# A graph layer on one core: rows of some chunks loaded one by one by two engines instead of one, and other sizes of the last node blocks

## The chip, the cores and the metric

The kernel runs on one core of one Trainium2 chip. The core has five engines, each with its own stream of instructions: TensorE (PE in the profile; PEld are its weight loads), VectorE (DVE), ScalarE (ACT), GpSimd (POOL) and SyncE (SP). SP computes nothing; it issues DMAs. ACT and POOL can issue DMAs as well. An instruction waits on semaphores, and what stands behind it on the same engine waits with it. The metric is the device time in microseconds (us); smaller is better.

## The reference, cut to what matters

There are N = 12500 nodes with D = 128 features and E = 200000 edges, sorted by destination. H is 512.

```python
h = jnp.maximum(_layernorm(x, axis=-1), 0.0)
msgs = h[src]                                            # one row of h per edge
agg = jax.ops.segment_sum(msgs, dst, num_segments=n)     # summed by destination
deg = jax.ops.segment_sum(jnp.ones((src.shape[0],), h.dtype), dst, num_segments=n)
agg = agg / jnp.maximum(deg, 1.0)[:, None]
y = jax.nn.relu(agg @ Wg + h @ Ws + bg)
y = jnp.tanh(y @ W1 + b1)
y = jnp.tanh(y @ W2 + b2)
out = x + (y @ W3 + b3)
```

Everything is float32.

## The kernel before

**Setup.** In nine pieces x is loaded, normalised on VectorE and ScalarE, and stored as the table `htab` in DRAM (lines 217 to 235). The edge lists are loaded, turned on TensorE and kept as one column per chunk: `scol` (sources) and `dloc` (destinations less the start of a window). GpSimd meanwhile runs 80 indirect DMAs of raw rows of x (line 142), which need no `htab`; these rows are normalised later on their own.

**Chunks.** The edges are cut into NCH = 1563 chunks of 128. A chunk's 128 source rows must be in SBUF, one per partition. They come in one of three ways:

- raw: 80 chunks, the gathers of line 142 from x;
- `gather(c)` (line 297): one indirect DMA on GpSimd from `htab`, with the indices of `scol[:, c]`. These chunks are listed in `order` (line 587), and 32 buffers (`AHEAD`) let it run 32 chunks ahead;
- slow: the chunks in the list `slow` (lines 84 to 91), one in every 81 that are not raw, from chunk 160. `row_loads` (line 314) loads their rows one by one: it reads 16 addresses from the tile `place` into registers of SP (line 320) and issues 16 DMAs of one 512-byte row each (line 327). It is a generator, and one call of `next(loading, 0)` in the main loop (line 639) issues one such batch of 16. Two buffers (`rows_one`) hold such chunks.

The addresses in `place` come from small loads of `src`, one per slow chunk, on ScalarE's queue (line 310).

**Sums.** As the destinations are sorted, chunk c touches only nodes near 8 * c. `window(c)` gives the start and the width of the window that its destinations must fall in (`WINDOWS`, line 49, narrower near the end). VectorE makes a one-hot matrix for eight chunks at a time (`onehot`, line 357), and `add(c)` (line 407) multiplies the rows by it on TensorE and sums into a block of nodes. A chunk that reaches two blocks is summed in `edge` first and handed to both by `merge`. One output, `flag`, says whether some destination fell outside its window; in that case `general`, a slower path, computes all again.

**Blocks and layers.** The nodes are cut into blocks (lines 103 to 107): 23 of 512, one of 256, three of 128 and a last one of 84. Once all chunks that reach a block are added, its dense layers can run: `part0` (agg and own rows through Wg and Ws, ReLU), `part1` (W1, tanh), `part2` (W2, tanh), `part3` (W3), `part4` (turned back, plus x, stored). They are generators as well.

**Order.** TensorE's instructions are kept in the order in which the code writes them (class `pe`, line 282), and so are SP's DMAs in the main loop (`sp_dma`). The main loop (line 616) goes over the chunks. For each it issues gathers up to 32 ahead, perhaps a batch of row loads, and `add(c)`. Up to chunk `QUICK` = 1376 it then does one step of the layers at every second chunk. From there on a small plan (`costs`, `soonest`, `go_on`, and `there`, the time at which a chunk's rows are expected) decides how many steps stand between two chunks. A block's layers begin `lead` chunks after its last chunk when it shares chunks with the next block: ten (`LEAD`) before `QUICK`, two after it. ScalarE's instructions are not held in written order.

Of the kernel before, what the change touches and what calls it, by code (L numbers as in the profile page):

```python
# [22 lines left out]
F32 = mybir.dt.float32  # L23
# [3 lines left out]
AF = mybir.ActivationFunctionType  # L27
# [4 lines left out]
P = 128  # L32
EPS = 1e-5
CPR = 16
BLK = 512
# [4 lines left out]
STEP = 40  # L40
AHEAD = 32
SLOW0 = 160
EACH = 80
LOADS = 16
LATE = 12
LEAD = 10
QUICK = 1376

WINDOWS = ((0, 144), (1496, 88), (1536, 56))
W_RAW = 160  # L50
W_MAX = max(W_RAW, *(w for _, w in WINDOWS))

# [6 lines left out]
def windowed(ctx, tc, x, src, dst, Wg, Ws, bg, W1, b1, W2, b2, W3, b3, out, flag):  # L59
    nc = tc.nc  # L60
    N, D = x.shape
# [9 lines left out]
    NCH = -(-E // P)  # L71
# [4 lines left out]
    assert D == P and H % P == 0 and per * E == N * P and RAW0 % GRP == STEP % GRP == 0  # L76
    assert all(c % GRP == 0 for c, _ in WINDOWS) and RAW1 <= WINDOWS[1][0]


    def raw(c):  # L80
        return RAW0 <= c < RAW1 and (c - RAW0) % STEP < GRP


    slow, n = [], 0
    for c in range(SLOW0, NCH - 100):
        if not raw(c):
            if n == 0:
                slow.append(c)
                n = EACH
            else:  # L90
                n -= 1


    def first(w, span=per):
# [6 lines left out]
        return per * c + first(w), w  # L101

    blocks, n = [], 0
    for w in [BLK] * (N // BLK - 1) + [BLK // 2] + [P] * 3:
        blocks.append((n, w))
        n += w
    blocks.append((n, N - n))

    dram = ctx.enter_context(tc.tile_pool(name="dram", bufs=1, space=bass.MemoryType.DRAM))
    const = ctx.enter_context(tc.tile_pool(name="const", bufs=1))  # L110
    raws = ctx.enter_context(tc.tile_pool(name="raws", bufs=1))
    rows_one = ctx.enter_context(tc.tile_pool(name="rows_one", bufs=2))
# [10 lines left out]
    for t, a in ((rsrc, src), (rdst, dst)):  # L123
        a = a[RAW0 * P : RAW1 * P].rearrange("(u e) -> u e", u=NRAW)[:, : GRP * P]
# [14 lines left out]
    for g in range(NRAW):  # L139
        t = raws.tile([P, GRP, D], F32, name=f"raw{g}")  # L140
# [44 lines left out]
    with tc.tile_pool(name="setup", bufs=1) as sp, tc.tile_pool(name="ln", bufs=2) as ln:  # L185
# [58 lines left out]
        )  # L244
        for c0, w in WINDOWS[1:]:
            v = low[:, c0:]
# [19 lines left out]
    bgc = const.tile([P, 1], F32, name="bgc")  # L266
    nc.scalar.dma_start(bgc, bg.rearrange("(p o) -> p o", o=1))
    b1c = const.tile([P, HM], F32, name="b1c")
    b2c = const.tile([P, HM], F32, name="b2c")
# [3 lines left out]
    b3c = const.tile([P, 1], F32, name="b3c")  # L273
# [20 lines left out]
    def sp_dma(*a):  # L294
        tc.keep_in_program_order(nc.sync.dma_start(*a))
# [10 lines left out]
    ROWB = 4 * D  # L306
    hbytes = htab.rearrange("n d -> (n d)").bitcast(U8)
# [3 lines left out]
    place = const.tile([len(slow), P], I32, name="place")  # L311
    nc.vector.tensor_scalar(place, at_i, float(ROWB), None, op0=ALU.mult)

    def row_loads():
        for i, c in enumerate(slow):
            r = rows_one.tile([P, D], F32, name="srows")
            rows_t[c] = r
            rb = r.bitcast(U8)
            for p0 in range(0, P, LOADS):
                loads, vs = nc.values_load_multi_w_load_instructions(  # L320
                    place[i : i + 1, p0 : p0 + LOADS], engines=[mybir.EngineType.SP], min_val=0, max_val=(N - 1) * ROWB,
                    skip_runtime_bounds_check_because="src holds rows of x, as the indirect DMAs take it to",
                )
                for ld in loads:
                    tc.keep_in_program_order(ld)
                for p, v in enumerate(vs, p0):
                    sp_dma(rb[p : p + 1, :], hbytes[bass.ds(v, ROWB)].rearrange("(o b) -> o b", o=1))
                yield

    def raw_stats(i):  # L330
        return stats_raw[:, :, i * GRP : (i + 1) * GRP]
# [39 lines left out]
    for c in range(NCH):  # L371
        lo, w = window(c)
# [28 lines left out]
    edge = {}  # L401
# [5 lines left out]
    def add(c):  # L407
        rows, oh = rows_t.pop(c), ohs[c // GRP][:, c % GRP]
        lo, w = window(c)
        b = min(b for b, cs in enumerate(reach) if c in cs)  # L410
        n, m = blocks[b]
        if c in across[b]:
            e0, e1 = edge_span(b)
            if c == across[b][0]:
                edge[b] = ps_b.tile([P, BLK], F32, name="edge")
            pe.matmul(
                edge[b][:, lo - e0 : lo - e0 + w], rows, oh[:, :w], start=(c == across[b][0]),
                stop=(c == across[b][-1]), skip_group_check=True,
            )
            if c == across[b][-1]:  # L420
                sums = ed.tile([P, BLK], F32, name="sums", bufs=2)
                nc.scalar.copy(sums[:, : e1 - e0], edge.pop(b)[:, : e1 - e0])
                edges[b] = sums
            return
        a0, a1 = max(lo, n), min(lo + w, n + m)
        if b not in acc:
            acc[b] = ps_a.tile([P, BLK], F32, name="agg")
            start = True
        else:
            start = False  # L430
        pe.matmul(
            acc[b][:, a0 - n : a1 - n], rows, oh[:, a0 - lo : a1 - lo], start=start,
            stop=(c == inside[b][-1] and not across[b]), skip_group_check=True,
        )
# [29 lines left out]
    def own_turned(s):  # L464

        k = -(-min(BLK, N - s * BLK) // P)
        hb = owns.pop(s)
        pt = ps_t.tile([P, BLK // P, P], F32, name="pt")
        for t in range(k):
            pe.transpose(pt[:, t, :], hb[:, t, :], ident)  # L470
        hT = ml.tile([P, BLK], F32, name="hT")
        nc.scalar.copy(hT[:, : k * P], pt[:, :k, :].rearrange("p t n -> p (t n)"))  # L472
        hTs[s] = hT

    def own_part(b):
# [15 lines left out]
    h0s, h1s, h2s, h3s = {}, {}, {}, {}  # L491
# [9 lines left out]
    def part0(b):  # L501
        n, mm, hop = costs(b)
        s, off = divmod(blocks[b][0], BLK)
        if n == BLK:
            own_part(b)
        yield 0, 0
        mT = ml.tile([P, BLK], F32, name="mT")
        nc.vector.tensor_tensor(mT[:, :n], acc[b][:, :n], rds.pop(b)[:, :n], op=ALU.mult)  # L508
        yield mm, 0
        p0 = flat(ps_m.tile([P, 4, P], F32, name="pm"))  # L510
        pe.matmul(p0[:, :n], ws, hTs[s][:, off : off + n], start=True, stop=False)
        yield mm, n / 90
        pe.matmul(p0[:, :n], wg, mT[:, :n], start=False, stop=True)
        h0s[b] = ml.tile([P, BLK], F32, name="h0")
        nc.scalar.activation(h0s[b][:, :n], p0[:, :n], AF.Relu, bias=bgc)  # L515

    def part1(b, spread):
        n, mm, hop = costs(b)
        size, bufs = wide(b)
        h0, h1s[b] = h0s.pop(b), ml.tile([P, HM, size], F32, name=f"h1_{size}", bufs=bufs)  # L520
        for m in range(HM):
            if spread and m > 1:
                yield 0, 0
            yield mm, hop if m == 0 else 0
            p1 = flat(ps_m.tile([P, 4, P], F32, name="pm"))
            pe.matmul(p1[:, :n], w1[:, m * P : (m + 1) * P], h0[:, :n], start=True, stop=True)
            nc.scalar.activation(h1s[b][:, m, :n], p1[:, :n], AF.Tanh, bias=b1c[:, m : m + 1])  # L527

    def part2(b):
        n, mm, hop = costs(b)  # L530
        size, bufs = wide(b)
        h1, h2s[b] = h1s.pop(b), ml.tile([P, HM, size], F32, name=f"h2_{size}", bufs=bufs)
        for m in range(HM):
            p2 = flat(ps_m.tile([P, 4, P], F32, name="pm"))
            for kk in range(HM):
                yield mm, hop if m == 0 and kk == HM - 1 else 0
                pe.matmul(
                    p2[:, :n], w2[:, kk, m * P : (m + 1) * P], h1[:, kk, :n], start=(kk == 0), stop=(kk == HM - 1)
                )
            nc.scalar.activation(h2s[b][:, m, :n], p2[:, :n], AF.Tanh, bias=b2c[:, m : m + 1])  # L540

    def part3(b):
        n, mm, hop = costs(b)
        h2 = h2s.pop(b)
        p3 = flat(ps_m.tile([P, 4, P], F32, name="pm"))
        for kk in range(HM):
            yield mm, hop if kk == HM - 1 else 0
            pe.matmul(p3[:, :n], w3[:, kk, :], h2[:, kk, :n], start=(kk == 0), stop=(kk == HM - 1))
        h3s[b] = ml.tile([P, BLK], F32, name="h3", bufs=1)
        nc.scalar.activation(h3s[b][:, :n], p3[:, :n], AF.Identity, bias=b3c)  # L550

    def part4(b):
        n0, (n, mm, hop) = blocks[b][0], costs(b)
# [31 lines left out]
        )  # L585

    order = [c for c in range(NCH) if not raw(c) and c not in slow]
    loading = row_loads()
    work, done, nxt, behind = [], 0, 0, 0
    ngrp = -(-NCH // GRP)  # L590
    span = BLK // per
# [24 lines left out]
    for c in range(NCH):  # L616
# [18 lines left out]
        if not raw(c) and c not in slow:  # L635
            behind += 1
            batch = behind * P // (EACH * LOADS)
            if behind > SLOW0 - 2 * EACH and batch > (behind - 1) * P // (EACH * LOADS):
                next(loading, 0)
        if c >= QUICK:  # L640

            there = 7.5 + 1.251 * (NRAW * GRP + order.index(c)) if c not in slow else 0
            while soonest() and max(now, soonest()[2]) < there:
                go_on(soonest())
            now = max(now, there) + 0.27
# [402 lines left out]
```

## Time and profile before

Three runs of the kernel took 1956.88 to 1958.13 us.

| what | us |
|---|---|
| median of three runs | 1957.18 |
| the profiled execution, by its own clock | 1961.69 |
| span of its trace, first to last instruction | 1959.50 |
| GpSimd busy | 1465.9 |
| TensorE busy | 1393.8 |
| VectorE busy | 1068.2 |
| ScalarE busy | 231.8 |
| one gather of line 299, mean | 0.946 |

All lines come from one profiled execution. A line of a group of instructions reads: source line, engine, operation, tiles written and read, count; then busy time in all and the mean of one in ns; then how long the engine sat idle just before these instructions, and what ended most of that. A line of the time line reads: start and length in us, engine, line, operation, and in square brackets the idle time before it with what ended it. An engine's name with a q, as in SPq, means its instruction queue: there the issue of DMAs is shown, which is not counted as busy. A row of digits cuts the span into 40 slices, and each digit is a share in tenths.

### The profile page before, as it was taken

The numbers are of one execution on the slowest core, as the hardware profiler recorded it, in microseconds if no ns is written. First come the engines' busy times: TensorE is split into PE (matmuls) and PEld (weight loads), VectorE is DVE, ScalarE is ACT, GpSimd is POOL, SyncE is SP. The second block draws the span as 40 slices with busy tenths as digits, with TensorE's granted clock in tenths as the row PEclk, the third lists the DMA queues.
The fourth block names the chain that finished last, engine by engine and source line by source line (L and its number), as shares of the span: only waits on it lengthen the run. The fifth ranks groups of instructions, "written<-read, shape, count | busy, mean of one in ns | idle before, by whom it ended". The sixth has DMA issues, their size and how long they took to land.

```text
span 1959.5 us, 19291 instructions
## 1 busy us (share of the span) xinstructions
PE 1393.8 (71%) x5213; PEld 824.1 (42%) x5213; DVE 1068.2 (55%) x650; ACT 231.8 (12%) x364; POOL 1465.9 (75%) x1555
## 2 busy tenths in 40 slices
PE   0056677777788778877777777777677677778897
PEld 0034344444454445533443434444343333454566
DVE  6974775555667656645545545455454554545430
ACT  1100211011111111010110110110001101101122
POOL 7777777777777777777777777777777777777774
PEclk9999778899989998899989888889889898879697
DMA  7822222222222222222222222222222222222221
GB/s 195 232 69 64 54 64 65 59 70 69 59 65 70 66 74 54 70 70 53 71 59 65 69 53 70 65 59 70 59 65 64 60 70 59 71 69 69 56 61 40
DMA packets 123684, 139.31 MB, mean 71 GB/s; under 512 B 32558, under 2 KB 97978, under 8 KB 123372
## 3 DMA queue, kind: packets, MB, share of 16 engines
q0 software_dynamic: 49504, 101.48, 20.4%
q1 hardware_dynamic: 70870, 33.19, 6.2%
q10 hardware_dynamic: 3192, 3.32, 0.6%
q8 instruction: 43, 0.70, 0.2%
q14 instruction: 75, 0.61, 0.1%
HBM read 125.05 MB, written 12.82 MB: 70 GB/s over the span
## 4 chain that ended last, share of the span: by engine, by line
DMA 36%; issue 28%; PE 26%; POOL 7%; DVE 3%; ACT 0%; SPq 0%; ACTq 0%; POOLq 0%; DVEq 0%
DMA rows<-htab,scol 34%; PE pm L286 13%; PE agg L286 9%; POOL rows L299 7%; PE edge L286 3%; DMA xt<-in_x_dram 2%; PE pt L289 1%; DMA at_i<-in_src_dram 0%; DVE oh L357 0%; DVE agg L176 0%; DVE h L183 0%; DVE agg L172 0%; DVE xt L173 0%; DVE cnt L367 0%; DVE shared L176 0%
## 5 line engine op out<-in xcount | busy, mean ns | idle before, releaser
L299 POOL DMA_INDIRECT rows<-htab,scol x1467 | 1387.6, 946 | 447.5 <-issue 269.3
L286 PE MATMUL agg<-oh,rows 128*128 128x144 f32 (+3 forms) x2096 | 560.2, 365 | 335.2 <-DMA rows<-htab,scol 324.3
L286 PEld LDWEIGHTS agg<-oh,rows 128*128 128x128 f32 x2096 | 381.9, 223 | 714.1 <-DMA rows<-htab,scol 597.5
L286 PE MATMUL pm<-h,w 128*128 128x512 f32 (+3 forms) x1344 | 639.0, 573 | 1.1 <-ACT h L515 0.7
L357 DVE TENSOR_TENSOR oh<-shared,dloc 128x1152 f32<-128x1152 f32 (+2 forms) x186 | 243.9, 1318 | 542.0 <-PE agg L286 330.6
L367 DVE TENSOR_REDUCE cnt<-oh 128x200 bf16<-128x1600 f32 (+2 forms) x186 | 524.3, 2824 | 4.6
L286 PE MATMUL edge<-oh,rows 128*128 128x144 f32 (+2 forms) x838 | 212.2, 346 | 124.3 <-DMA rows<-htab,scol 123.8
L286 PEld LDWEIGHTS edge<-oh,rows 128*128 128x128 f32 x838 | 145.0, 210 | 277.1 <-DMA rows<-htab,scol 242.3
L286 PEld LDWEIGHTS pm<-h,w 128*128 128x128 f32 x1344 | 219.8, 202 | 15.2 <-issue 12.0
L540 ACT ACTIVATE h<-pm,b2c 128x512 f32<-128x512 f32 (+3 forms) x112 | 70.9, 633 | 554.8 <-PE pm L286 554.8
L527 ACT ACTIVATE h<-pm,b1c 128x512 f32<-128x512 f32 (+3 forms) x112 | 70.5, 633 | 237.4 <-PE pm L286 236.9
L142 POOL DMA_INDIRECT raw<-in_x_dram,rsrc x80 | 77.4, 967 | 25.5 <-issue 23.8
L394 DVE RECIPROCAL rd<-rd 128x512 f32<-128x512 f32 (+3 forms) x28 | 81.8, 2920 | 0.0
L564 DVE TENSOR_TENSOR o<-pt,xb 128x512 f32<-128x512 f32 x23 | 15.9, 690 | 95.7 <-PE pt L289 91.9
L508 DVE TENSOR_TENSOR mT<-agg,rd 128x512 f32<-128x512 f32 (+3 forms) x28 | 17.4, 620 | 86.6 <-PE agg L286 86.6
L201 PE MATMUL pm<-ident,idx_f 98*128 98x98 f32 x32 | 6.2, 376 | 64.2 <-DVE idx_f L197 57.8
L392 DVE TENSOR_SCALAR rd<-pm 128x512 f32<-128x512 f32 (+3 forms) x28 | 17.4, 622 | 61.6 <-PE pm L286 61.6
L515 ACT ACTIVATE h<-pm,bgc 128x512 f32<-128x512 f32 (+3 forms) x28 | 17.7, 633 | 271.8 <-PE pm L286 271.8
L472 ACT COPY hT<-pt 128x512 f32<-128x512 f32 (+1 forms) x25 | 14.4, 578 | 258.5 <-PE pt L289 246.9
L286 PE MATMUL pm<-hT,ws 128*128 128x512 f32 (+3 forms) x56 | 41.2, 831 | 0.0
L550 ACT ACTIVATE h<-pm,b3c 128x512 f32<-128x512 f32 (+3 forms) x28 | 17.7, 633 | 181.9 <-PE pm L286 181.9
L289 PE MATMUL pt<-ident,hb 128*128 128x128 f32 x98 | 16.6, 297 | 31.5 <-DMA srows<-htab 31.5
(69 smaller groups left out, 499.1 us busy)
## 6 DMA issues: line engine op xcount, KB each, us to landing
srows<-htab SPq DMA_DIRECT2D x2048, 0.5 KB
rows<-htab,scol POOLq DMA_INDIRECT x1467, 2.5
hb<-htab SPq DMA_DIRECT2D x24, 256.0 KB
xb<-in_x_dram SPq DMA_DIRECT2D x23, 256.0 KB
out_dram<-o SPq DMA_DIRECT2D x23, 256.0 KB
htab<-h SPq DMA_DIRECT2D x6, 896.0 KB
xt<-in_x_dram SPq DMA_DIRECT2D x5, 896.0 KB
raw<-in_x_dram,rsrc POOLq DMA_INDIRECT x80, 3.9
```

The source lines that it names most:

```text
L142: nc.gpsimd.indirect_dma_start(out=t[:, j, :], out_offset=None, in_=x, in_offset=bass.IndirectOffsetOnAxis(ap=rsrc[:, g, j : j + 1], axis=0),)
L286: tc.keep_in_program_order(nc.tensor.matmul(*a, **k))
L289: tc.keep_in_program_order(nc.tensor.transpose(*a, **k))
L299: nc.gpsimd.indirect_dma_start(out=r, out_offset=None, in_=htab, in_offset=bass.IndirectOffsetOnAxis(ap=scol[:, c : c + 1], axis=0),)
L357: nc.vector.tensor_tensor(oh[:, :k, :w], lane[:, None, :w].to_broadcast([P, k, w]), dloc[:, g * GRP : g * GRP + k][:, :, None].to_broadcas ...
L367: nc.vector.tensor_reduce(cnt[:, :n], shifted, AX.X, ALU.add)
L392: nc.vector.tensor_scalar(rd[:, :m], dg[:, :m], 1.0, None, op0=ALU.max)
L394: nc.vector.reciprocal(rd[:, :m], rd[:, :m])
L515: nc.scalar.activation(h0s[b][:, :n], p0[:, :n], AF.Relu, bias=bgc)
L527: nc.scalar.activation(h1s[b][:, m, :n], p1[:, :n], AF.Tanh, bias=b1c[:, m : m + 1])
L540: nc.scalar.activation(h2s[b][:, m, :n], p2[:, :n], AF.Tanh, bias=b2c[:, m : m + 1])
L550: nc.scalar.activation(h3s[b][:, :n], p3[:, :n], AF.Identity, bias=b3c)
```

## The change

1. **Two lists of slow chunks.** `slow` becomes `slow_s` (for SP, one in every 77) and `slow_a` (for ScalarE, one in every 121, up to `QUICK`). SP's list now goes on to 12 chunks before the end, not 100.
2. **ScalarE loads rows.** `row_loads` takes the list, the engine, the function that issues a DMA, the name of the tile, and how many loads go out per call. For SP this is 16 as before; for ScalarE four (`TOGETHER`), with addresses still read 16 at a time. The main loop calls ScalarE's generator in its own rhythm.
3. **ScalarE's order is held.** A class `act` keeps its activations, copies and row loads of the main loop in written order.
4. **Other last blocks.** The last blocks are 256, 128, 128, 112 and 100 instead of 256, 128, 128, 128 and 84, and from chunk 1552 on the window is 40 wide instead of 56.

```diff
-EACH = 80
+EACH = 76
+EACH_A = 120
+TOGETHER = 4
...
-WINDOWS = ((0, 144), (1496, 88), (1536, 56))
+WINDOWS = ((0, 144), (1496, 88), (1536, 56), (1552, 40))
...
-    slow, n = [], 0
-    for c in range(SLOW0, NCH - 100):
-        if not raw(c):
-            if n == 0:
-                slow.append(c)
-                n = EACH
-            else:
-                n -= 1
+    slow_s, slow_a = [], []
+    ns, na = 0, EACH // 2
+    for c in range(SLOW0, NCH - 12):
+        if raw(c):
+            continue
+        if ns <= 0:
+            slow_s.append(c)
+            ns = EACH
+        elif na <= 0 and c < QUICK:
+            slow_a.append(c)
+            na = EACH_A
+        else:
+            ns -= 1
+            na -= 1
+    slow = slow_s + slow_a
...
-    for w in [BLK] * (N // BLK - 1) + [BLK // 2] + [P] * 3:
+    for w in [BLK] * (N // BLK - 1) + [BLK // 2] + [P] * 2 + [P - 16]:
...
+    class act:
+        def activation(*a, **k):
+            tc.keep_in_program_order(nc.scalar.activation(*a, **k))
+        def copy(*a):
+            tc.keep_in_program_order(nc.scalar.copy(*a))
+        def dma(*a):
+            tc.keep_in_program_order(nc.scalar.dma_start(*a))
-    def row_loads():
-        for i, c in enumerate(slow):
-            r = rows_one.tile([P, D], F32, name="srows")
+    def row_loads(chunks, engine, dma, name, together):
+        for c in chunks:
+            i = slow.index(c)
+            r = rows_one.tile([P, D], F32, name=name)
...
-                    sp_dma(rb[p : p + 1, :], hbytes[bass.ds(v, ROWB)].rearrange("(o b) -> o b", o=1))
-                yield
+                    dma(rb[p : p + 1, :], hbytes[bass.ds(v, ROWB)].rearrange("(o b) -> o b", o=1))
+                    if (p + 1) % together == 0:
+                        yield
...
-    loading = row_loads()
+    loading = row_loads(slow_s, mybir.EngineType.SP, sp_dma, "srows", LOADS)
+    loading_a = row_loads(slow_a, mybir.EngineType.Activation, act.dma, "arows", TOGETHER)
...
+            batch = behind * P // (EACH_A * TOGETHER)
+            if behind > 48 and batch > (behind - 1) * P // (EACH_A * TOGETHER):
+                next(loading_a, 0)
```

The activations and copies of the layers (lines 422, 472, 515, 527, 540 and 550) call `act.activation` and `act.copy` in place of the engine's own.

More of the change, by code (lines that the diff above doesn't have):

```diff
@@ L107, in windowed @@
     blocks.append((n, N - n))
+    assert 0 < N - n <= P
     dram = ctx.enter_context(tc.tile_pool(name="dram", bufs=1, space=bass.MemoryType.DRAM))
@@ L320, in row_loads @@
                 loads, vs = nc.values_load_multi_w_load_instructions(
-                    place[i : i + 1, p0 : p0 + LOADS], engines=[mybir.EngineType.SP], min_val=0, max_val=(N - 1) * ROWB,
+                    place[i : i + 1, p0 : p0 + LOADS], engines=[engine], min_val=0, max_val=(N - 1) * ROWB,
                     skip_runtime_bounds_check_because="src holds rows of x, as the indirect DMAs take it to",
@@ L421, in add @@
                 sums = ed.tile([P, BLK], F32, name="sums", bufs=2)
-                nc.scalar.copy(sums[:, : e1 - e0], edge.pop(b)[:, : e1 - e0])
+                act.copy(sums[:, : e1 - e0], edge.pop(b)[:, : e1 - e0])
                 edges[b] = sums
@@ L471, in own_turned @@
         hT = ml.tile([P, BLK], F32, name="hT")
-        nc.scalar.copy(hT[:, : k * P], pt[:, :k, :].rearrange("p t n -> p (t n)"))
+        act.copy(hT[:, : k * P], pt[:, :k, :].rearrange("p t n -> p (t n)"))
         hTs[s] = hT
@@ L514, in part0 @@
         h0s[b] = ml.tile([P, BLK], F32, name="h0")
-        nc.scalar.activation(h0s[b][:, :n], p0[:, :n], AF.Relu, bias=bgc)
+        act.activation(h0s[b][:, :n], p0[:, :n], AF.Relu, bias=bgc)
     def part1(b, spread):
@@ L526, in part1 @@
             pe.matmul(p1[:, :n], w1[:, m * P : (m + 1) * P], h0[:, :n], start=True, stop=True)
-            nc.scalar.activation(h1s[b][:, m, :n], p1[:, :n], AF.Tanh, bias=b1c[:, m : m + 1])
+            act.activation(h1s[b][:, m, :n], p1[:, :n], AF.Tanh, bias=b1c[:, m : m + 1])
     def part2(b):
@@ L539, in part2 @@
                 )
-            nc.scalar.activation(h2s[b][:, m, :n], p2[:, :n], AF.Tanh, bias=b2c[:, m : m + 1])
+            act.activation(h2s[b][:, m, :n], p2[:, :n], AF.Tanh, bias=b2c[:, m : m + 1])
     def part3(b):
@@ L549, in part3 @@
         h3s[b] = ml.tile([P, BLK], F32, name="h3", bufs=1)
-        nc.scalar.activation(h3s[b][:, :n], p3[:, :n], AF.Identity, bias=b3c)
+        act.activation(h3s[b][:, :n], p3[:, :n], AF.Identity, bias=b3c)
     def part4(b):
```

## The prediction

> **What bounds the kernel now.** I read the busy shares first, then the groups of instructions, then the time line of GpSimd and of the end.
>
> ```profile
> PE 1393.8 (71%) x5213; PEld 824.1 (42%) x5213; DVE 1068.2 (55%) x650; ACT 231.8 (12%) x364; POOL 1465.9 (75%) x1555
> ...
> DMA  7822222222222222222222222222222222222221
> ...
> L299 POOL DMA_INDIRECT rows<-htab,scol x1467 | 1387.6, 946 | 447.5 <-issue 269.3
> ```
>
> GpSimd is 75% busy, but the third line says why that is full: each of its 1467 gathers takes 946 ns and is followed by 447.5 / 1467 = 305 ns in which nothing can start. "issue" as the largest releaser means that it waited for nothing that the profile shows. Does it ever wait for a free buffer? The first and the last gather of the time line answer:
>
> ```profile
> 98.46 0.95 POOL L142 DMA_INDIRECT raw<-in_x_dram,rsrc  x1 [0.31 <-DMA htab<-h]
> ...
> 104.73 0.95 POOL L299 DMA_INDIRECT rows<-htab,scol  x1 [0.30 <-DVE cnt L367]
> 105.98 0.95 POOL L299 DMA_INDIRECT rows<-htab,scol  x1 [0.30 <-issue]
> ...
> 1938.59 0.95 POOL L299 DMA_INDIRECT rows<-htab,scol  x1 [0.30 <-POOLq L1014]
> ```
>
> (1938.59 - 104.73) / 1466 = 1.2509 us a gather, and the longest single step between two gathers in the trace is 1.27 us. So GpSimd never waits, from the raw gathers before 104.73 to the last. The reader is to see that the whole kernel is one queue of gathers with a start before it and a tail behind it. TensorE follows 2.5 us behind each gather, with buffers for 32 of them.
>
> **Gathers taken off GpSimd.** Working through the loop that fills the lists of row-by-row chunks gives 16 chunks before; after, 17 on the sync engine and 9 on ScalarE, 26 together. The sum of chunks is 1563, of which 80 are raw: 1563 - 80 - 26 = 1457 gathers against 1467. Ten fewer at 1.2509 us are **-12.5 us**, all of it on the path that sets the end.
>
> Here a rule of the Trainium skill speaks against the change: "DMA: Bandwidth & Descriptors", section "Rules for kernel authors", says that spreading DMAs over SP, ACT and GpSimd brings no bandwidth, as all run on the same 16 engines; it saves issue time only. If the transfers were the bound, the gain would be 0. The row for DMA above shows 2 tenths busy after the start, and issue time is what GpSimd is full of, so the exception in that rule is this case: 12.5 us, not 0.
>
> **What ScalarE gets.** 9 x 128 = 1152 loads of one 512-byte row, four at a time, 288 batches between chunks 48 and 1225 of the loop. No row load of ScalarE is in this trace; the nearest row is the sync engine's:
>
> ```profile
> 786.99 0.41 SPq L295 DMA_DIRECT2D out_dram<-o  x1
> 789.29 11.63 SPq L295 DMA_DIRECT2D srows<-htab  x32
> 801.02 0.40 SPq L295 DMA_DIRECT2D hb<-htab  x1
> ```
>
> 32 loads with one read of addresses take 11.63 us, 0.363 each; so 1152 take 418 us, 1.45 a batch. The other end is ScalarE's 16 loads of index rows at the start (33.92 to 45.40 us, 0.72 each, under full DMA traffic): 829 us. I take 0.363, since these loads lie in the stage with little traffic. ScalarE has 231.8 us of work in 1959, so it has room. What matters is who waits for ScalarE meanwhile. Queued behind a batch are its copies and activations, and behind those TensorE. In the list of waits for TensorE between 700 and 1100 us no wait for ScalarE exists:
>
> ```profile
> PE agg L286 <- DMA rows<-htab,scol: 73.1, 104, 2.1
> PE edge L286 <- DMA rows<-htab,scol: 26.5, 35, 2.3
> PE agg L286 <- DVE oh L357: 1.5, 1, 1.5
> PE agg L286 <- DVE o L564: 0.5, 1, 0.5
> ```
>
> The code says how far that carries: up to chunk 1376 one step of the layers is issued every two chunks (2.5 us), a result of ScalarE is read three or more steps later, an edge sum ten chunks later. A batch of 1.45 us fits in that. What is still late is bought back: TensorE is busy 895.7 of the 1200 us from 300 to 1500, a quarter free, and GpSimd feels nothing until TensorE is 32 x 1.25 - 2.5 = 37 us behind. Cost **0**. Without this cover it would be the 418 us, less 25% idle time over the some 1470 us of that stage (373) and the 37 of buffers: 8. Behind chunk 1225 ScalarE has no loads, so the tail is clean.
>
> A wait comes with it. Each DMA of SP and of ACT names one of the same eight semaphores in turn and waits until the eighth DMA before it, whosever it was, has landed. Eight of SP's loads take 8 x 0.323 = 2.6 us and none waits in the row above, so a row lands within that; the gathers land in 2.5. ScalarE can thus stand up to about 2.5 us behind SP's batch, at most once for each of SP's 17 x 8 = 136 batches, and SP can't run far ahead of ScalarE. Below: no wait, since SP's program is ahead of TensorE's; above: 136 x 2.5 = 340 us on ScalarE. I take 0 on the path, by the same cover.
>
> **SP's share**, 17 chunks instead of 16, spaced 76 instead of 80: 128 x 0.363 = 46 us of loading in 76 x 1.25 = 95. Their last load lies 70 chunks and more ahead of use. Nothing.
>
> **The start.** Ten more of the small index loads on ScalarE's queue stand ahead of work of the normalisation. At their median, 0.26, they are 2.7 us; at 0.72 they are 7.2, and one more turn of the eight semaphores (one such wait lasted 3.9 us, to 38.39) makes 11. The last store to htab had landed by 98.7, while GpSimd was on raw gathers until 104.73: 6.0 us are free. Loss 0 to 5; I take **0**.
>
> **The tail.** Narrower windows from chunk 1552 let the second-last block (112 nodes) end its chunks at 1551 instead of 1554.
>
> ```profile
> 1943.72 0.30 PE L286 MATMUL agg<-oh,rows 128*128 128x28 f32 x2
> 1943.83 1.64 PEld L286 LDWEIGHTS pm<-h,w 128*128 128x128 f32 x14
> ...
> 1944.06 0.25 DVE L508 TENSOR_TENSOR mT<-agg,rd 128x84 f32<-128x84 f32 x1 [8.78 <-PE agg L286]
> ...
> 1946.80 5.79 PE L286 MATMUL pm<-h,w 128*128 128x84 f32 x48
> ```
>
> The last chunk had landed by 1938.59 + 2.5 = 1941.1, yet TensorE adds it at 1943.7 and begins the last block's hidden layers at 1946.80, 8.2 us after the last gather began, because the block before stands ahead in its order. Working the written order out again with the new reaches, that block's products all stand ahead of the last chunk's, and after it comes only the last block: 2.5 landing, 0.43 for the add, 0.3 for mT, 0.35 for wg, 0.4 for ReLU and its hand-over, 4.1 us in all with 0.1 for gaps. Gain 8.2 - 4.1 = 4.1. The clock stood at half from 1931.8 to 1942.0; should it stand so there again, the block before ends some 1 us late (gain 3), and where the old kernel ran at full clock there, its own lead was some 2.5 us shorter (gain 1.5). I take **-3.0**. The last block is 100 wide instead of 84: its 48 matmuls are bound by weight loads (1.64 / 14 = 117 ns at 128 columns, 5.79 / 48 = 121 at 84), four activations in series grow by 0.015 each: **+0.1**. Sixteen fewer columns for eleven chunks: nothing (0.30 us at 28 columns, 0.31 at 36).
>
> **Sum.** -12.5 - 3.0 + 0.1 = -15.4. The profiled execution took 1961.69 (span 1959.50 and 2.19 around it), so it would take 1946.3. The runs shown have a median 4.5 below it; off 1957.18 it is **1941.8 us**, 0.8% less.
>
> **Rivals.** (1) The start is late: 11 us against 6.0 free, a loss of 5, **1947**. For it: one such semaphore wait already stands there; against it: DVE has idle time there as well. (2) The clock is halved under the last 48 matmuls (ten took 2.46 at half clock, so 11.8 instead of 5.7): **1948**. For it: 22% of the trace is at half clock; against: TensorE is steadily busy just before. (3) Row loads slow GpSimd's gathers by 10 ns each: 1457 x 10 = 14.6, **1956**, no change. Against: the pitch was 1.2510 with SP's loads about and 1.2506 after they ended at 1680. (4) ScalarE becomes the bound, **slower**: 418 us of issue and 340 of semaphore waits all stop TensorE: 758 - 373 - 37 = 348, less 15.4, about **2290**. It decides from 425 us on TensorE's path, 1.48 a batch. For it: TensorE's order is fixed, and one late result stops all chunks behind it; against: the list of waits. That the change fails to do what it says, a destination outside a 40-wide window so that the general path runs as well, is out: in the drawn inputs the nearest destination lies 14 nodes inside.
>
> **Numbers.** Forecast 0.68 (own range 1939 to 1944.5), (1) 0.12, (2) 0.07, (3) 0.04, (4) 0.09. A measurement of this kernel tells 0.2%, 3.9 us, from no change. Faster: 0.68 + 0.10 of (1) + 0.07 = 0.85; same: 0.02 of (1) and 0.03 of (3) = 0.05; slower: 0.01 of (3) and (4) = 0.10. The range takes in (1) and (2): 1938.5 to 1949; what it leaves out are (3) and (4) and edges.
>
> **What would show it.** Right: 1457 gathers at 1.251 us, the first at 104.7, the last at 1926.1; 1152 row loads on ACT's queue with TensorE's waits for ScalarE still absent; last hidden layers some 4 to 5 us behind the last gather's start. Wrong: gaps between gathers over 1.27 us (TensorE over 37 us behind), waits of TensorE for ScalarE in the middle stage, or a first gather after 105.

## The result and the profile after

| | us |
|---|---|
| changed kernel, median of four runs (1942.12 to 1944.14) | 1943.25 |
| kernel before, median of four runs beside them | 1957.03 |
| ratio, with its 95% interval | 0.9929 [0.9918, 0.9941] |
| span of the changed kernel's trace | 1940.2 |

The kernel became 13.8 us faster; 15.4 were forecast, and the forecast of 1941.8 is 1.5 below the measured time. First GpSimd, in the group of the gathers and in the time line of its first and last one:

```profile
L310 POOL DMA_INDIRECT rows<-htab,scol x1457 | 1374.7, 944 | 444.4 <-issue 256.2
```

```profile
103.29 0.94 POOL L153 DMA_INDIRECT raw<-in_x_dram,rsrc  x1 [0.30 <-issue]
104.54 0.94 POOL L310 DMA_INDIRECT rows<-htab,scol  x1 [0.30 <-issue]
...
1922.37 0.94 POOL L310 DMA_INDIRECT rows<-htab,scol  x1 [0.30 <-DMA rows<-htab,scol]
```

There are 1457 gathers, still back to back (no step over 1.27 us), and the first one still follows directly on the raw gathers, so the ten further index loads on ScalarE's queue delayed nothing. The last gather starts 16.2 us earlier than in the trace before. Ten gathers are 12.5 of that. The rest is the pitch: (1922.37 - 104.54) / 1456 = 1.2485 us, against 1.2509. All six later traces in which GpSimd never waits, one with the old 1467 gathers among them, have 1.2484 to 1.2486. The one profiled execution of the kernel before ran its gathers 0.2% slower (some 3.7 us over 1547 of them), which would be most of the 4.5 us by which it lay above the median of the other runs. So the two spans, 19.3 us apart, overstate the gain.

TensorE's waits in the middle stage (110 to 1700 us; in all, times, longest, in us) and SP's:

```profile
PE agg L297 <- DMA rows<-htab,scol: 259.4, 410, 2.4
PE pt L300 <- DMA hb<-htab: 120.7, 16, 12.8
...
PE pm L297 <- ACT h L329: 12.7, 1, 12.7
PE agg L297 <- ACT sums L332: 5.2, 1, 5.2
```

```profile
SPq L306 <- DMA arows<-htab: 599.5, 242, 41.0
SPq L306 <- DVE o L589: 178.4, 6, 61.1
```

This is new. The trace's records name the same eight semaphores for the DMAs of SP and of ScalarE, and each DMA waits for the one before it on its own semaphore. So SP stood 599.5 us behind row loads of ScalarE, up to 41 us at once, and `hb`, the block of own rows that SP loads, then came late for TensorE's transposes 16 times, 120.7 us in all. Why this cost nothing is the question of the experiments.

The end of the changed kernel, all in one time line:

```profile
1925.90 0.32 PE L300 MATMUL pt<-ident,h 128*112 128x128 f32 x1 [0.29 <-ACT h L329]
...
1926.06 0.30 PE L297 MATMUL agg<-oh,rows 128*128 128x20 f32 x2
...
1927.67 5.85 PE L297 MATMUL pm<-h,w 128*128 128x100 f32 x48 [0.43 <-ACT h L329]
```

The second-last block's transpose now stands ahead of the last chunk's product, so the order is the one worked out. The last hidden layers begin 1927.67 - 1922.37 = 5.3 us behind the last gather's start, where it had been 8.2.

### The profile page after: what moved, and what is told of

Read it like the earlier page. It is cut to its first block, busy times and chain, and to the rows that moved or that the text cites. A ratio compares the mean times of both kernels' runs of the same rounds, so it can differ in the third digit from the quotient of the medians.

```text
span 1940.2 us, 21950 instructions
## 1 busy us (share of the span) xinstructions
PE 1353.0 (70%) x5212; PEld 829.8 (43%) x5212; DVE 1067.5 (55%) x651; ACT 228.8 (12%) x362; POOL 1452.7 (75%) x1545
## 4 chain that ended last, share of the span: by engine, by line
PE 30%; DMA 27%; issue 23%; POOL 9%; SPq 8%; DVE 2%; ACTq 1%; ACT 1%; POOLq 0%
DMA rows<-htab,scol 23%; PE pm L297 17%; PE agg L297 8%; SPq L306 6%; POOL rows L310 5%; PE edge L297 5%; POOL raw L153 4%; DMA hb<-htab 2%; SPq L344 2%; DMA arows<-htab 1%; PE pt L300 1%; ACTq L335 1%; DVE cnt L392 1%; ACT h L329 0%; DVE oh L382 0%
## 5 line engine op out<-in xcount | busy, mean ns | idle before, releaser
L297 PE MATMUL agg<-oh,rows 128*128 128x144 f32 (+3 forms) x2086 | 534.9, 358 | 288.0 <-DMA rows<-htab,scol 279.1
L297 PE MATMUL pm<-h,w 128*128 128x512 f32 (+4 forms) x1344 | 643.3, 575 | 14.2 <-ACT h L329 14.1
L297 PE MATMUL edge<-oh,rows 128*128 128x144 f32 (+2 forms) x828 | 186.4, 332 | 54.9 <-DMA rows<-htab,scol 54.3
L300 PE MATMUL pt<-ident,hb 128*128 128x128 f32 x98 | 23.4, 385 | 153.1 <-DMA hb<-htab 120.7
L329 ACT ACTIVATE h<-pm,b2c 128x512 f32<-128x512 f32 (+4 forms) x112 | 70.8, 632 | 447.4 <-PE pm L297 415.3
L329 ACT ACTIVATE h<-pm,b1c 128x512 f32<-128x512 f32 (+4 forms) x112 | 70.5, 632 | 227.4 <-PE pm L297 206.6
L419 DVE RECIPROCAL rd<-rd 128x512 f32<-128x512 f32 (+4 forms) x28 | 81.8, 2920 | 0.0
L332 ACT COPY hT<-pt 128x512 f32<-128x512 f32 (+1 forms) x25 | 14.4, 577 | 363.6 <-PE pt L300 348.5
L417 DVE TENSOR_SCALAR rd<-pm 128x512 f32<-128x512 f32 (+4 forms) x28 | 17.3, 618 | 61.5 <-PE pm L297 61.5
L329 ACT ACTIVATE h<-pm,bgc 128x512 f32<-128x512 f32 (+4 forms) x28 | 17.7, 632 | 245.6 <-PE pm L297 245.6
L297 PE MATMUL pm<-hT,ws 128*128 128x512 f32 (+4 forms) x56 | 41.2, 831 | 0.0
L533 DVE TENSOR_TENSOR mT<-agg,rd 128x512 f32<-128x512 f32 (+4 forms) x28 | 17.3, 617 | 39.6 <-PE agg L297 39.5
```

The source lines that it names most:

```text
L297: tc.keep_in_program_order(nc.tensor.matmul(*a, **k))
L300: tc.keep_in_program_order(nc.tensor.transpose(*a, **k))
L329: tc.keep_in_program_order(nc.scalar.activation(*a, **k))
L417: nc.vector.tensor_scalar(rd[:, :m], dg[:, :m], 1.0, None, op0=ALU.max)
L419: nc.vector.reciprocal(rd[:, :m], rd[:, :m])
```

## The experiments

Two theories came out of the result. **A**: time is gathers times pitch, and ScalarE's loads cost nothing; as 12.5 of 13.8 us are the gathers, the tail gave about 1. **B**: the tail gave the 2.9 us that the two traces show, and ScalarE's loads took some of the gathers' gain back.

### The parts alone

Change without the tail's edits:

```diff
-WINDOWS = ((0, 144), (1496, 88), (1536, 56), (1552, 40))
+WINDOWS = ((0, 144), (1496, 88), (1536, 56))
...
-    for w in [BLK] * (N // BLK - 1) + [BLK // 2] + [P] * 2 + [P - 16]:
+    for w in [BLK] * (N // BLK - 1) + [BLK // 2] + [P] * 3:
```

> The change without the other block sizes and the 40-wide window: ScalarE's nine chunks and SP's 17 stay. Theory A (time is the number of gathers times their pitch, and ScalarE's loads cost nothing): ten gathers fewer at 1.249 us, 12.5 us under the kernel before, 1944.5. Theory B (ScalarE's loads take some of it back): less than 11 us under it, 1946 or more. Last gather's start to the end of the span as before, some 20.9 us.

The other way about, the kernel before with these two edits alone:

> The kernel before with the new block sizes and windows alone: 1467 gathers. Theory A leaves 13.8 - 12.5 = 1.3 us for the tail: 1955.7. Theory B leaves the 2.9 us by which the changed kernel's last gather stands nearer to its first hidden layer: 1954.1.

The changed kernel without ScalarE's chunks:

```diff
+    slow_a = []
     slow = slow_s + slow_a
```

> The changed kernel without ScalarE's nine chunks, which are gathered again: 1466 gathers, tail as changed. Theory A: 9 x 1.249 = 11.2 us above the changed kernel, 1954.5. Theory B: less than that above it, since ScalarE's loads no longer cost: 1952 to 1953.

The changed kernel with ScalarE's loads issued but their rows not used; the nine chunks are gathered (`order` leaves out `slow_s` only, and two tests in the main loop name `slow_s` in place of `slow` as well):

```diff
-            rows_t[c] = r
+            if name == "srows":
+                rows_t[c] = r
...
-    order = [c for c in range(NCH) if not raw(c) and c not in slow]
+    order = [c for c in range(NCH) if not raw(c) and c not in slow_s]
```

> ScalarE loads the rows of its nine chunks, but nothing reads them: these chunks are gathered as well. 1466 gathers as in the run without ScalarE's chunks. Theory A: the same time as that run within 2 us, 1954.5, since 1152 loads on ScalarE's queue lie under the gathers. Theory B: 2 us or more above that run.

| run | gathers | median us | to the kernel before, 1956.7 | ratio and interval |
|---|---|---|---|---|
| loads only | 1457 | 1944.42 | -12.3 | 0.9936 [0.9923, 0.9950] |
| tail only | 1467 | 1957.53 | +0.8 | 1.0003 [0.9994, 1.0011] |
| no chunks on ScalarE | 1466 | 1955.92 | -0.8 | 0.9993 [0.9987, 1.0000] |
| ScalarE's loads unused | 1466 | 1955.83 | -0.9 | 0.9994 [0.9985, 1.0002] |

The last two differ by 1152 loads on ScalarE's queue and by 0.1 us of time. Their intervals would hide a cost of some 2 us, but the traces are sharper: from the first gather to the last, over the same 1465 steps, it is 1829.05 us without these loads and 1829.10 with them. So the loads cost nothing. Loads alone give 12.3 us for ten gathers. B falls. But the tail gives less than A left for it as well. Alone it shows no gain at all. The two kernels with 1466 gathers should lie 1.2 us under the kernel before for their one gather less, and lie 0.8 and 0.9 under it, so the new tail gains nothing there either. What it adds to the loads, 1944.42 - 1943.25 = 1.2 us, lies within the intervals.

### Where ScalarE's loads went

The waits of TensorE, 110 to 1700 us, in the last two runs, first without loads on ScalarE, then with loads that nobody reads:

```profile
PE agg L298 <- DMA rows<-htab,scol: 294.6, 445, 2.0
PE edge L298 <- DMA rows<-htab,scol: 101.5, 152, 1.8
PE pm L298 <- ACT h L330: 12.7, 1, 12.7
```

```profile
PE agg L297 <- DMA rows<-htab,scol: 269.5, 421, 2.0
PE pt L300 <- DMA hb<-htab: 113.2, 15, 13.0
PE edge L297 <- DMA rows<-htab,scol: 39.7, 62, 1.4
```

The waits for `hb` come with the loads; the single wait for ScalarE doesn't, it stands in both (11.5 us in the second). So the loads do hold TensorE up. Pairing each gather with the product that reads its rows gives TensorE's lag: between gathers 200 and 1100 it reaches 9.5 us without loads on ScalarE and 18.1 with them (19.8 in the changed kernel). TensorE stood waiting for rows a quarter of that stretch without these loads (294.6 and 101.5 us of 1590), so it makes the lag good, and GpSimd has the 37 us of buffers that the prediction worked out. Four runs try this cover from both sides: more loads, and fewer buffers.

```diff
-EACH_A = 120
+EACH_A = 60
...
-            r = rows_one.tile([P, D], F32, name=name)
+            r = rows_one.tile([P, D], F32, name=name, bufs=2 if name == "srows" else 5)
```

> ScalarE's list with one chunk in 61 instead of 121: 18 chunks, 1448 gathers, five buffers for them. Theory A (loads stay under the gathers while TensorE's lag, up to 20 us in the changed kernel, stays under 37): nine gathers fewer, 11.2 us under the changed kernel, 1932. Theory B (the lag grows with the loads, to some 40 us): it shows gaps over 1.3 us between gathers and gains less, 1935 to 1960.

With `EACH_A = 40` and six buffers:

> One chunk in 41 on ScalarE: 27 chunks, 1439 gathers, six buffers. 27 x 46.5 us = 1255 us of loads in some 1470 us beside ScalarE's own work. Theory A: still hidden, 22.5 us under the changed kernel, 1921. Theory B: ScalarE sets the pace of that stage, gaps between gathers, slower than the kernel before: 1960 or more.

With `AHEAD = 10` in place of 32, in the changed kernel and in the one without chunks on ScalarE:

> The changed kernel with 10 buffers for gathered rows instead of 32: TensorE may lag 10 us, not 37. Theory A' (ScalarE's loads do hold TensorE up, and the buffers hide it): the lags over 10 us that the trace of the changed kernel has between 300 and 1520 us come out as gaps, 40 us or more above the run with 10 buffers and no loads on ScalarE. Theory C (no result of ScalarE is ever late): 11 us under that run.

> The run without ScalarE's chunks, with 10 buffers for gathered rows. Both theories: the lags of 20 us at the start and of 20 us near chunk 1376, which stand in its trace too, come out as some 20 us: 1976.

None of the four can be held against the numbers expected, because the kernel before itself took 2290 us on this chip, 17% more (what is slow there stands in the last section). They can be compared with each other. GpSimd is not the bound there: in these four traces 200 to 261 of its steps take over 1.3 us, up to 23.7, and most of that time ends with an instruction of TensorE, which frees a buffer. So hold-ups of TensorE show in the time.

| run on that chip | us |
|---|---|
| kernel before | 2290.16 |
| 10 buffers, no chunks on ScalarE | 2279.59 |
| 10 buffers, nine chunks on ScalarE | 2435.12 |
| 32 buffers, 18 chunks on ScalarE | 2472.62 |
| 32 buffers, 27 chunks on ScalarE | 2797.34 |

Nine chunks on ScalarE cost 155.5 us there, although they take nine gathers away. The trace with them has the wait seen above, TensorE's for `hb`, 18 times and 310.1 us in all; the one without them has none. That is A' in kind: where nothing covers TensorE's hold-ups, the loads are not free. The size expected for a chip of the usual pace stays untested. So 18 chunks were run again, on a chip on which the kernel before took 1957.10:

> The run with 18 chunks on ScalarE once more, since the kernel before took 2290 us on the chip of the first one, where TensorE was the bound. Where the kernel before takes some 1957, theory A (TensorE's lag stays under 37 us): 1932. Theory B (the lag grows past 37 us with twice the loads): gaps over 1.3 us between gathers, and a gain lost in part or in whole, 1935 to 1980.

It took 1935.43 us, 0.9893 [0.9878, 0.9908] of the kernel before: faster than both kernels. The number lies between the two theories, at the edge of B's range; the gathers decide. Its gathers, and its last one in the time line:

```profile
L310 POOL DMA_INDIRECT rows<-htab,scol x1448 | 1366.3, 944 | 441.7 <-DMA rows<-htab,scol 198.3
```

```profile
1911.13 0.94 POOL L310 DMA_INDIRECT rows<-htab,scol  x1 [0.30 <-DMA rows<-htab,scol]
...
1917.58 7.46 PE L297 MATMUL pm<-h,w 128*128 128x100 f32 x48 [0.43 <-ACT h L329]
```

No step between the gathers of `htab` is over 1.3 us, the lag stays at 20, and the last gather starts at 1922.37 - 9 x 1.2485 = 1911.13, to the hundredth. A holds for the gathers. Some 3 of the 3.4 us by which it misses 1932 lie behind the last gather: 20.8 us from its start to the end, where the changed kernel's trace has 17.8, with the same code in that stretch. So the tail is not one number.

What holds TensorE up is no longer the same, though. In this trace it does not wait for `hb` between 110 and 1700 us, but for ScalarE, whose activations stand behind its own row loads:

```profile
PE pm L297 <- ACT h L329: 119.0, 42, 12.3
PE agg L297 <- ACT sums L332: 50.0, 10, 9.4
```

```profile
ACT h L329 <- DMA arows<-htab: 605.4, 101, 26.5
```

With twice the loads ScalarE's results do come late, and only the cover of idle time and buffers keeps that from the gathers.

### What sets the tail

Busy time by stretches of the last part (columns: stretch, its length, busy us with counts for PE, PEld, DVE, ACT, POOL, then the granted TensorE clock, DMA share, GB/s), of the changed kernel and of the run without chunks on ScalarE. In each the first of the two stretches ends about at the last gather:

```profile
1900.00:1923.00 23.00, 19.90 (x128) 18.98 (x128) 1.85 (x7) 6.38 (x18) 17.52 (x19) 0.77 0.22 57
1923.00:1940.00 17.00, 9.98 (x80) 9.03 (x79) 0.75 (x3) 4.28 (x13) 0.31 (x1) 0.93 0.07 17
```

```profile
1911.00:1934.00 23.00, 20.58 (x116) 20.01 (x117) 1.85 (x7) 5.84 (x17) 17.51 (x19) 0.65 0.23 58
1934.00:1957.00 23.00, 15.86 (x90) 14.90 (x88) 0.75 (x3) 4.64 (x14) 0.08 (x1) 0.72 0.05 11
```

Same blocks, same order, but a granted clock of 0.77 and 0.93 in the one and 0.65 and 0.72 in the other, with 17.8 and 23.9 us from the last gather's start to the end. Where the half clock falls, ten products of the block before take 2.45 us, not 1.35, and the last chunks wait behind them (the changed kernel, then the run without chunks on ScalarE):

```profile
1922.10 1.35 PE L297 MATMUL pm<-h,w 128*128 128x112 f32 x10
```

```profile
1934.34 2.45 PE L298 MATMUL pm<-h,w 128*128 128x112 f32 x10
```

That accounts for the difference: in the second run the last hidden layers begin 4.4 us later after the last gather's start, and a second spell makes their 48 products 1.6 us longer. The next table has the spells of all the traces, by the records of the granted clock, up to the end of TensorE's work.

| run | half clock around the last gather's start, us | its start to the end, us |
|---|---|---|
| before | -6.8 to 3.4 | 20.9 |
| changed | -8.5 to -1.7 | 17.8 |
| loads only (old tail) | -8.3 to 1.9 | 20.0 |
| tail only | -9.1 to 1.1, 8.0 to 11.4 | 21.2 |
| no chunks on ScalarE | -9.5 to 7.5, 10.9 to 14.4 | 23.9 |
| ScalarE's loads unused | -7.3 to 3.0 | 20.0 |
| 18 chunks | -9.6 to 0.6, 7.4 to 10.9 | 20.8 |

The new order saves time, and the half clock takes it, in some runs more than it saves. The run with ScalarE's loads unused is the plainest case: its spell falls within half a us of that of the kernel before, and its last hidden layers begin 1940.88 - 1933.48 = 7.4 us behind the last gather's start.

```profile
1940.88 5.85 PE L297 MATMUL pm<-h,w 128*128 128x100 f32 x48 [0.43 <-ACT h L329]
```

With the old order and that spell it was 8.2. So the new order is worth 0.8 us there, and 2.9 in the changed kernel's trace, whose spell ended 4.7 us earlier. The second spell, under the last hidden layers, stands in three of the five traces with the new order and in neither with the old one.

The runs scatter accordingly: 1953.0 to 1959.2 in 21 runs without chunks on ScalarE, 1953.7 to 1960.3 in 13 of the tail alone, but 1955.6 to 1958.4 in 41 of the kernel before. So the four runs of the changed kernel say little of what its tail is worth on average.

What brings the spells? The clock's records change on a grid of 3.4 us. From 25 us before the last gather to the end of the work, the clock in these traces is halved only after a stretch of that length which products filled by 27 to 77%. "TensorE: Matmul & The Clock Gate" of the Trainium skill (section "Part 1: The HAM clock gate") says that activity releases the throttle. That can be tried, with spare products in TensorE's idle stretches (`steps` counts the steps of the layers since the last chunk, and `BUSY0` is 1500):

```diff
+        if c > BUSY0:
+            for _ in range(4 - steps):
+                p = flat(ps_m.tile([P, 4, P], F32, name="pm"))
+                pe.matmul(p[:, :P], ident, ident, start=True, stop=True)
+        steps = 0
         add(c)
```

> The changed kernel, but from chunk 1501 on TensorE gets spare products of the identity with itself wherever fewer than four steps of the layers stand between two chunks; nothing reads them. Theory T (the tail's length is set by where the clock is halved, and TensorE's idle stretches bring that about): no half clock in the last 40 us, last gather's start to the end of the span 17 us or less, time 1 to 3 us under the changed kernel. Theory U (the halving has nothing to do with idle stretches): the spells stay, and the spare products only delay the last blocks: no change or up to 5 us more.

```profile
1850.00:1900.00 50.00, 49.54 (x318) 42.02 (x317) 13.78 (x20) 8.45 (x18) 37.75 (x40) 1.00 0.22 61
1900.00:1923.00 23.00, 22.05 (x192) 21.21 (x191) 3.85 (x10) 6.27 (x19) 17.29 (x19) 1.00 0.20 56
1923.00:1954.00 31.00, 23.55 (x200) 22.51 (x200) 2.69 (x10) 7.03 (x22) 0.64 (x1) 0.92 0.05 14
```

The clock is 1.00 up to the end of the work (0.92 takes in the idle end), so the spells do go with idle stretches. The 13 runs lie within 1.8 us, 1954.6 to 1956.3, so the scatter goes with the spells too. The page's sentence fits this trace, but a spell's end is less regular than it sounds: without spare products full clock came back after one to four filled stretches of 3.4 us, after four in the run without chunks on ScalarE. But it took 1955.59 us: four spare products and an add fill a gather's 1.25 us, and beside the wide blocks' steps before chunk 1526 they exceed it. TensorE was some 15 us behind when the last gather landed. T held for the clock and fell for the time, so that a held clock shortens the tail is not shown by a run; it rests on the lengths of the same products at the two clocks. A lighter filling, three steps from chunk 1529 on, was tried with 18 and with 27 chunks on ScalarE:

> 18 chunks on ScalarE, and from chunk 1529 on spare products on TensorE wherever fewer than three steps of the layers stand between two chunks (three of them and an add take 1.03 us of a gather's 1.25, so no lag can build up). Theory T (idle stretches bring the half clock, and the half clock sets the tail): no half clock in the last 20 us before the last hidden layers, last gather's start to the end 17 us, last gather at 1911: 1930. Theory U (the spare products help nothing): a tail of 20 us or more as in the run without them, 1934 to 1936.

> The same with 27 chunks on ScalarE and 1439 gathers. Theory A (TensorE's lag still stays under 37 us): no gaps, last gather at 1900, 1919. Theory B (three times the loads fill ScalarE, TensorE falls more than 37 us behind): gaps over 1.3 us between gathers, above the run with 18 chunks, 1935 or more.

They ran on another chip of the slow kind (kernel before 2291.06) and took 2482.08 and 2788.57 us, about what the two without filling had taken. Whether the light filling shortens the tail, and whether 27 chunks still fit on a chip of the usual pace, stays open.

## Why the prediction was right, and where not

- **Ten gathers off GpSimd, -12.5.** Right in count, pitch and place: 12.3 us with the loads alone. The gain came from time to issue, the one gain that the rule cited in the prediction leaves to spread DMAs.
- **ScalarE's loads, cost 0.** Right, shown by the loads that nobody reads. The reason was only half right. The prediction expected that a batch of 1.45 us fits between the steps of the layers, and looked at waits for ScalarE. Those were few, until the loads were doubled. What came was its other sentence, that SP can't run far ahead of ScalarE: through the shared semaphores SP fell back, and `hb` with it. The bound of 2.5 us a wait was put on ScalarE's side; SP's side had waits of up to 41 us and had no number. What saved the step was the second cover, the idle time and the 37 us of buffers.
- **SP's share, nothing.** Its own chunks came in time, but "nothing" holds for the time alone, for the same reason.
- **The start, 0.** Right: first gather at 104.54.
- **The tail, -3.0 + 0.1.** This is the term that was mis-sized. The order came out as worked out, and in the trace the last layers stand 2.9 us nearer. But in the time it is worth 1.2 us beside the loads and -0.8 alone, neither clear of 0. The step that failed is the cost of the half clock. The prediction put it at some 1 us should the spell fall where it fell before, for a gain of 3; where it did so the gain was 0.8, under the least it allowed, 1.5. It also let the spell fall where it fell in one trace, but it moves between runs, and a second one can come. That the changed kernel's trace shows nearly the 3.0 is luck of its spell, which ended early.
- **Rivals.** (1) did not happen. (2), the half clock under the last 48 products, happened in part in three of these tails (7.46 to 7.48 us for 48 products, not 5.85). The share of half clock that spoke for it is 20% of the trace by the mean clock of 0.901, not 22%. (3) did not: 1.2485. (4) did not on chips of the usual pace, though its way, one late result stops all chunks, is what a slow chip shows with 18 chunks: TensorE waited 290.0 us for ScalarE's activations there and 158.3 for its copies (110 to 2200 us).

## What to carry to other kernels

Where one queue is full from start to end, an instruction taken off it is worth its pitch (ten gathers gave 12.3 us, and ten times the pitch is 12.5), and another engine's queue costs nothing as long as the engine that consumes both has idle time and buffers to make good its hold-ups; count those, not the engine's busy share. DMAs of two engines that share a ring of semaphores tie the queues to each other, so ask what else stands on the faster queue. And a gain at the tail read from one trace is worth little where a clock spell of its size can fall on it: time it alone, and often.

## What the runs showed of the hardware

**Chips differ.** On two of the four chips on which experiments ran the kernel before took 2290 us, not 1957. GpSimd's gathers last the same there (943 to 946 ns). The instructions of SP show where to look. These are its register moves, with shortest, median and longest in ns, with 18 chunks on ScalarE on a chip of the usual pace, then on a slow one:

```profile
L306 SPq MOVE srows<-htab x2176: 29/29/37, 97.9 to 1709.3; - x198
```

```profile
L306 SPq MOVE srows<-htab x2176: 1/29/1427, 104.8 to 2237.6; - x198
```

A move takes 29 ns at the median on both, but up to 1427 on the slow chip. What delays it was not measured: the packets by which instructions are loaded, which the traces hold as well, last no longer there (505 ns at the median, against 484). On such a chip ScalarE's loads are no gain: 18 chunks cost 8% there and saved 1.1% elsewhere. The changed kernel itself was not run on one.

**Order has a price too.** The wait of 12.7 us for ScalarE near the start stands, at 11.5 to 12.7 us, in the changed kernel and in the runs with loads only, without ScalarE's chunks and with its loads unused. It is not in the kernel before and not in the run of the tail alone, where ScalarE's instructions were not held in written order. No run takes out that order alone, so it is the likely cause and not a shown one. The lag of 20 us that comes with it is made good without a gap between gathers.
